# Turning the experts' hidden layer on its side: through memory, or block by block out of PSUM

## Chip, cores and metric

The kernel runs on one core of one Trainium2 chip. The metric is the device time of one execution in microseconds (us); the kernel before takes 285.71 us in the median of three runs (285.37 to 286.24).

## What is computed

A graph layer and a mixture of experts follow one another over 625 nodes of width 1024. The graph layer gathers neighbours by relation, projects them, applies an ELU, projects back and adds the result. The change touches only the mixture of experts:

```python
x = x + gnn(layernorm(x), edges, ...)
xf = layernorm(x)                                   # 625 x 1024
sh = gelu(xf @ sW1[i] + sb1[i]) @ sW2[i] + sb2[i]   # 2 shared experts, their mean
gates = xf @ rW + rb                                # 8 experts, the best 2 for each row
h = gelu(xf @ W1[e] + b1[e])                        # hidden width 256
y = h @ W2[e] + b2[e]
x = x + mean(sh) + sum_e w[t, e] * y[e, t]          # w: softmax over the best 2
```

## The kernel before, in words

All of it is one program whose instruction order on each engine is laid out ahead of time by the planner of the framework: of the instructions whose inputs it holds to be ready, it takes the earliest in program order. `tc.issue_after(a)` puts what is issued inside it behind `a` on `a`'s engine.

The graph layer fills the first 119 us. Then come the shared experts' first products (p_sh, L1146), with gating and routing between them. Routing sorts the chosen (row, expert) pairs into 11 tiles of 128 slots. In order of work the tiles are 4, 5, 6, 0, 7, 1, 8, 2, 9, 10, 3; below, "the first" to "the eleventh" tile counts in this order. Tiles 4 to 10 belong to one expert each. Tiles 0, 1 and 2 are split in two halves of 64 slots, tile 3 in four quarters of 32, with an expert for each part.

For each tile the loop `for s in range(NJ + 2)` (L1557) does this:

- `gather` (GpSimd) fetches 128 rows of 1024 from memory into one of three buffers, with four transfers for the tiles in `by_quarters` (first, second, fourth, sixth, eighth, tenth) and one for the others.
- `fetch` and `turn` bring the features to the partitions (xsT, two buffers). For the tiles in `by_quarters`, VectorE turns the whole tile at once (L1485). For the others TensorE turns it in two halves of four blocks (p_x, L1496); ScalarE evicts the first half (L1502), VectorE the second (L1500). The second half belongs to the next pass of the loop.
- `copy_w1` (ScalarE, L1509) copies first-layer weights for the split tiles.
- `expert_in` multiplies (p_h, L1515): 8 blocks of features, traced as 16 matmuls for a whole tile. The result is 128 slots by 256 hidden values in one PSUM bank; three banks serve these. The first four blocks need only the first half of xsT, the last four also the second.
- VectorE copies p_h to `hj` in SBUF, one buffer (L1519). SyncE's queue sends hj to `hd` in memory (L1521), and, with the next tile, four transfers of 32 KB bring it back to `hjT` (`to_quarters`, L1528), which moves each block of 32 hidden values to its own quarter of the partitions.
- `expert_mid`, at pass s for the tile s - 4, lets VectorE turn the 32x32 blocks inside each quarter (hT, L1537) and ScalarE apply bias and GELU back into hjT (L1542). L1537 is put behind the last copy of p_h.

`expert_out` (p_yj, L1578) multiplies the hidden values by W2, 512 columns to a PSUM bank, in the order 4, 5, 6, 0, 1, 2, 3, 7, 8, 9, 10. Its first two banks stand ahead of the closing of the pools `xts` and `in_w`; the other tiles follow in a loop with the copies of second-layer weights for split tiles (w2m, ScalarE, L1608), the evictions (ys, L1618 on VectorE and L1620 on ScalarE) and the scatters into `yt` (GpSimd, L1625). The last three `expert_mid` stand in that loop. On SyncE's queue, the loads of the shared experts' second weights (sw2, L1592) stand behind the last write of hd, then `to_quarters` of the last two tiles, then the loads of x1 (L1599).

Last come the shared experts' second products (p_o, L1676 and L1678), the weighted sums on VectorE (L1647) and the stores.

Of the kernel before, what the change touches and what calls it, by code (L numbers as in the profile page):

```python
# [8 lines left out]
F32 = mybir.dt.float32  # L9
# [14 lines left out]
H = 256  # L24
NE = 8
NS = 2
TP = 125
# [16 lines left out]
NJ = 11  # L44
# [9 lines left out]
HK = H // 128  # L54
# [399 lines left out]
def sparse_kernel(  # L454
# [24 lines left out]
    nc = tc.nc  # L479

    def pool(stack, name, bufs=1, side="left", **kw):
        return stack.enter_context(tc.tile_pool(name=name, bufs=bufs, side=side,
                                                reuse_waits="tile", **kw))
# [5 lines left out]
    dram = ctx.enter_context(tc.tile_pool(name="dram", bufs=1, space=bass.MemoryType.DRAM))  # L489
    h2d = dram.tile([N, D], F32, name="h2d")  # L490
    x1d = dram.tile([N, D], F32, name="x1d")
    hd = dram.tile([NJ, 128, H], F32, name="hd")

    yt = dram.tile([2 * YB, D], F32, name="yt")

    def ps_acc(name):
        return psum[0].tile([128, 512], F32, tag="acc", name=name, bufs=nacc[0])

    def ps_mm(name):
        return psum[0].tile([128, 512], F32, tag="mm", name=name, bufs=3)  # L500
# [279 lines left out]
    def first_row():  # L780
        x0 = xh[:TP, 0, :]
        h = rows.tile([TP, D], F32, tag="h", name="h_0")
        part = fbig.tile([TP, 3], F32, name="part")
        with tc.issue_after(behind.ins):
            nc.vector.tensor_reduce(part[:, 0:1], x0[:, :HALF], axis=AX.X, op=ALU.add)
        with tc.issue_after(table.ins):
            nc.scalar.activation(h[:, HALF:], x0[:, HALF:], AF.Identity, accum_out=part[:, 1:2])
        last = nc.vector.tensor_scalar(part[:, 2:3], part[:, 0:1], part[:, 1:2], -1.0 / D, op0=ALU.add, op1=ALU.mult)
        moved = nc.scalar.activation(h[:, :384], x0[:, :384], AF.Identity, bias=part[:, 2:3])
        with tc.issue_after(last.ins):  # L790
            last = nc.vector.tensor_scalar(h[:, 384:], x0[:, 384:], part[:, 2:3], None, op0=ALU.add)
        hs[0] = h
        return last, moved
# [264 lines left out]
    last, moved = first_row()  # L1058
# [122 lines left out]
    def load_w2(e):  # L1181
        nc.sync.dma_start(w2a[:, e], W2[e].rearrange("(k p) d -> p k d", p=128))
# [261 lines left out]
    mid = pool(ctx, "mid")  # L1444
    hjT = mid.tile([128, NJ, HK, 128], F32, name="hjT")
    xts = ExitStack()
    xt = pool(xts, "xt", 2, side="right")
# [5 lines left out]
    def parts(j):  # L1453
        if j < NH2:
            return (0, HS, e_of[j]), (HS, 128, e_of[NH2 + j])
        if j < NM2:
            return [(QS * i, QS * (i + 1), e_of[nt + i]) for i in range(4)]
        return ((0, 128, e_of[NH2 + j - 1]),)

    xsT, w1m, copied, moved = {}, {}, [], []  # L1460
    acts = []

    rows = {}
# [29 lines left out]
    def turn(j, g):  # L1493
        p = ps_acc(f"p_x{g}_{j}")
        for k in range(4):
            nc.tensor.transpose(p[:, k * 128 : (k + 1) * 128], half_row[j][:, 4 * g + k :: KD], ident)  # L1496
        o = xsT[j][:, 4 * g : 4 * g + 4, :]
        pv = p.rearrange("p (k n) -> p k n", k=4)
        if g:
            turned.append(nc.vector.tensor_copy(o, pv))  # L1500
        else:
            acts.append(nc.scalar.copy(o, pv))  # L1502
# [8 lines left out]
    def expert_in(j):  # L1511
        p = ps_mm(f"p_h_{j}")
        for k in range(KD):
            for a, b, e in parts(j):
                nc.tensor.matmul(p[a:b, :H], xsT[j][:, k, a:b],  # L1515
                                 w1m[j, a][:, 0, k, :] if a else w1a[:, bass.ds(e, 1), k, :],
                                 start=(k == 0), stop=(k == KD - 1))
        h = xt.tile([128, H], F32, tag="hj", bufs=1, name=f"hj_{j}")
        copied.append(nc.vector.tensor_copy(h.rearrange("p (q c r) -> p c q r", q=4, c=HK),  # L1519
                                           p[:, :H].rearrange("p (c q r) -> p c q r", c=HK, q=4)))  # L1520
        moved.append(nc.sync.dma_start(hd[j], h))  # L1521
        if j not in (tiles[0], tiles[-1]):
            with tc.issue_after(moved[-1].ins):
                to_quarters(tiles[tiles.index(j) - 1])

    def to_quarters(j):
        for q in range(4):
            nc.sync.dma_start(hjT[32 * q : 32 * q + 32, j].rearrange("t c (b r) -> t (c b r)", b=4)  # L1528
                              .rearrange("t (b x) -> t b x", b=4),
                              hd[j].rearrange("(b t) (q x) -> q t b x", b=4, q=4)[q])  # L1530

    bT = vT[:, KD + NS * HK :].rearrange("p (e t) -> p e t", t=HK)

    def expert_mid(j):
        p = mid.tile([128, HK, 128], F32, tag="hT", name=f"hT_{j}")
        with tc.issue_after(copied[-1].ins):
            nc.vector.transpose(p.rearrange("p c (b t) -> p c b t", b=4),  # L1537
                                hjT[:, j].rearrange("p c (b r) -> p (c b r)", b=4)
                                .rearrange("p (b c r) -> p c b r", b=4, c=HK))
        for t in range(HK):  # L1540
            for a, b, e in parts(j):
                done = nc.scalar.activation(hjT[:, j, t, a:b], p[:, t, a:b], AF.Gelu,  # L1542
                                     bias=bT[:, bass.ds(e, 1), t])
        acts.append(done)
# [3 lines left out]
    tiles = (*whole[:3], 0, whole[3], 1, whole[4], 2, *whole[5:], NH2)  # L1548
# [8 lines left out]
    for s in range(NJ + 2):  # L1557
        if 0 < s <= NJ and tiles[s - 1] in half_row:
            turn(tiles[s - 1], 1)
        if s < NJ:  # L1560
            if s > 2:
                rows[tiles[s]] = io.tile([128, D], F32, tag="io", name=f"xs_{tiles[s]}")
                gather(tiles[s])
            fetch(tiles[s])
        if 0 <= s - 1 < NJ:
            expert_in(tiles[s - 1])
        if s == 2:
            load_w2(NE - 1)
        if 0 <= s - 4 < NJ - 3:
            expert_mid(tiles[s - 4])  # L1570
    ORDER = (*whole[:3], *range(NM2), *whole[3:])
    w2m, p_ys = {}, {}

    def expert_out(j, s):
        p_ys[j, s] = p = ps_acc(f"p_yj_{j}_{s}")
        for k in range(HK):
            for a, b, e in parts(j):
                made = nc.tensor.matmul(p[a:b], hjT[:, j, k, a:b],  # L1578
                                        (w2m[j, a, k] if a else w2a[:, bass.ds(e, 1), k])[..., s * 512 : (s + 1) * 512],
                                        start=(k == 0), stop=(k == HK - 1))  # L1580
        return made

    for s in range(2):
        expert_out(ORDER[0], s)
    xts.close()
    in_w.close()

    late = pool(ctx, "late", side="right")
    sw2 = late.tile([128, NS, HK, D], F32, name="sw2")
    for i in range(NS):  # L1590
        with tc.issue_after(moved[-1].ins):
            last = nc.sync.dma_start(sw2[:, i], sW2[i].rearrange("(k p) d -> p k d", p=128))  # L1592
    with tc.issue_after(last.ins):
        to_quarters(tiles[-2])
        to_quarters(tiles[-1])
    x1 = late.tile([TP, NT, D], F32, name="x1")
    for a, b in ((0, 3), (3, NT)):
        with tc.issue_after(last.ins):
            nc.sync.dma_start(x1[:, a:b], x1d[a * TP : b * TP].rearrange("(t p) d -> p t d", p=TP))  # L1599
    gat = pool(ctx, "gat", 15, side="right")  # L1600

    loads, (off,) = nc.values_load_multi_w_load_instructions(flag, min_val=0, max_val=EC * 4 + 1)
# [7 lines left out]
    for n, j in enumerate(ORDER):  # L1610
        y = gat.tile([128, D], F32, tag="y", name=f"ys_{j}")
        for s in range(2):
            at = slice(s * 512, (s + 1) * 512)
            if n:
                made = expert_out(j, s)
            p = p_ys[j, s]
            if s or n < 4:
                copied.append(nc.vector.tensor_copy(y[:, at], p))  # L1618
            else:
                nc.scalar.copy(y[:, at], p)  # L1620

        if n < 3:
            expert_mid(tiles[n - 3])

        sent.append(nc.gpsimd.indirect_dma_start(  # L1625
            out=yt, out_offset=bass.IndirectOffsetOnAxis(ap=row[:, j : j + 1], axis=0), in_=y, in_offset=None,
            bounds_check=2 * YB - 1, oob_is_err=False))
        for s in sent[:-1]:
            tc.declare_no_dep(sent[-1].ins, s.ins, reason="rows of different slots")

    gs = {}
    for d in range(NT):
        for a in range(2):
            at = a * YB + 1 + d * TP
# [29 lines left out]
    for d in range(NT):  # L1664
        if LATE < d < NT - 1:
            add_rows(d)
        own = slice(d * TP, (d + 1) * TP)
        for at in ((0, 512), (512, D)) if d < NT - 1 else ((0, 512), (512, 768), (768, D)):
            n = at[1] - at[0]
            at = slice(*at)  # L1670
            p = (ps_mm if banks % 8 > 4 else ps_acc)(f"p_o_{d}_{at.start}")
# [59 lines left out]
```

## Time and profile before

| what | value |
|---|---|
| median of 3 runs | 285.71 us (285.37 to 286.24) |
| the profiled execution | 285.32 us, its span 283.5 us |
| granted TensorE clock | 0.997 of full speed |
| busy: TensorE matmul / VectorE / ScalarE / GpSimd | 274.4 / 175.7 / 101.8 / 61.1 us |
| instructions: matmul / VectorE / ScalarE / GpSimd | 1509 / 446 / 232 / 122 |
| p_h (L1515), first to last matmul | 158.37 to 203.8 us |
| hj copy (L1519) / hT turn (L1537) | 11 of 421 ns / 11 of 436 ns |
| DMA issues of SyncE for hd and hjT | 11 and 44 |

The span is the time between the first and the last instruction of the trace; 1.8 us lie around it. "Busy" is the time in which an engine had an instruction; matmuls overlap, and their ends are modelled. A "releaser" is what ended an engine's idle time. All positions are microseconds from the start of the span.

### The profile page before, as it was taken

How to read it: one execution, taken by the hardware profiler on the slowest of the kernel's cores; microseconds unless marked ns; L12 is line 12 of the kernel's file. 1: busy time of each engine (PE TensorE's matmuls, PEld its weight loads, DVE VectorE, ACT ScalarE, POOL GpSimd, SP SyncE). 2: the span in 40 equal slices, each digit the busy share in tenths (PEclk: the TensorE clock that was granted, in tenths of full speed). 3: DMA queues.
4: the chain of work that ended last, by engine and by line, in shares of the span. 5: the costliest groups of instructions: out<-in, count | busy, mean ns of one | idle time of the engine just before them, and what ended most of it. 6: DMA issues, size and time to landing. Idle time of an engine off the chain costs nothing.

```text
span 283.5 us, 4565 instructions
## 1 busy us (share of the span) xinstructions
PE 274.4 (97%) x1509; PEld 183.3 (65%) x1509; DVE 175.7 (62%) x446; ACT 101.8 (36%) x232; POOL 61.1 (22%) x122
## 2 busy tenths in 40 slices
PE   8899999999999999999999999799999999999993
PEld 7667777788888655677777787678544324444452
DVE  4889999999975689838930641555341312216972
ACT  2347326534642242445101150856298311100000
POOL 9810020000000032210047555360020222210000
PEclk9999999999999999999999999999999999999998
DMA  7999981000000899998999279754296554439962
GB/s 226 356 324 355 371 289 47 2 0 2 1 0 2 322 369 425 420 375 321 390 415 393 88 221 283 202 154 137 68 329 217 218 205 191 186 115 385 392 219 79
DMA packets 29987, 64.48 MB, mean 227 GB/s; under 512 B 8961, under 2 KB 16196, under 8 KB 28935
## 3 DMA queue, kind: packets, MB, share of 16 engines
q1 hardware_dynamic: 24475, 48.74, 47.9%
q0 software_dynamic: 5200, 15.04, 15.1%
q10 hardware_dynamic: 284, 0.35, 0.4%
q8 instruction: 14, 0.23, 0.3%
q14 instruction: 14, 0.11, 0.1%
HBM read 44.63 MB, written 20.26 MB: 229 GB/s over the span
## 4 chain that ended last, share of the span: by engine, by line
PE 82%; DMA 8%; DVE 7%; SPq 1%; issue 0%; ACT 0%; DVEq 0%
PE p_pr L956 15%; PE p_yj L1578 14%; PE p_o L1676 12%; PE p_sh L1146 12%; PE p_h L1515 10%; PE p_y L1031 6%; PE p_agg L985 5%; DMA xh<-in_x_dram 4%; DMA hd<-hj 4%; DVE st L777 2%; PE cnt L934 2%; PE p_t L844 2%; DVE ohs L903 1%; PE p_x L1496 1%; PE p_gate L1198 1%; PE p_y L1032 1%
## 5 line engine op out<-in xcount | busy, mean ns | idle before, releaser
L956 PE MATMUL p_pr<-wg,nT 128*125 128x286 f32 x240 | 62.4, 410 | 0.9 <-DVE neg L798 0.6
L956 PEld LDWEIGHTS p_pr<-wg,nT 128*125 128x125 f32 x240 | 43.3, 187 | 13.4 <-ACT nT L850 1.2
L1578 PE MATMUL p_yj<-w2a,hjT 128*128 (+2 forms) x88 | 38.7, 595 | 0.0
L1676 PE MATMUL p_o<-sw,shT 128*125 128x512 f32 (+1 forms) x88 | 36.3, 553 | 0.0
L1146 PE MATMUL p_sh<-h2T,sw 128*128 128x313 f32 (+1 forms) x128 | 35.3, 429 | 0.0
L1515 PE MATMUL p_h<-w1a,xsT 128*128 (+2 forms) x144 | 32.7, 380 | 1.5 <-DVE xsT L1485 1.5
L1578 PEld LDWEIGHTS p_yj<-w2a,hjT 128*128 128x128 f32 (+2 forms) x88 | 14.5, 168 | 23.3 <-issue 22.8
L1146 PEld LDWEIGHTS p_sh<-h2T,sw 128*128 128x128 f32 x128 | 23.6, 189 | 8.5 <-issue 0.2
L1515 PEld LDWEIGHTS p_h<-w1a,xsT 128*128 128x128 f32 (+2 forms) x144 | 22.8, 163 | 7.7 <-issue 1.7
L1676 PEld LDWEIGHTS p_o<-sw,shT 128*125 128x125 f32 x88 | 16.4, 187 | 16.9 <-issue 15.9
L1468 POOL DMA_INDIRECT xs<-h2d,tok x24 | 22.7, 946 | 19.0 <-issue 5.8
L1618 DVE COPY ys<-p_yj 128x512 f32<-128x512 f32 x15 | 10.3, 689 | 26.1 <-PE p_yj L1578 26.1
L1625 POOL DMA_INDIRECT yt<-ys,row x11 | 10.7, 970 | 48.9 <-DVE ys L1618 48.9
L1519 DVE COPY hj<-p_h 128x256 f32<-128x256 f32 x11 | 4.6, 421 | 24.5 <-PE p_h L1515 19.0
L1031 PE MATMUL p_y<-wo_t,eT 128*125 128x512 f32 (+1 forms) x40 | 18.8, 592 | 0.0
L1042 POOL DMA_DIRECT2D x1d<-xh x4 | 2.2, 542 | 65.6 <-DVE flagf L727 62.1
L1542 ACT ACTIVATE hjT<-hT,vT 128x128 f32<-128x128 f32 (+2 forms) x34 | 9.8, 354 | 17.1 <-DVE hT L1537 10.2
L985 PE MATMUL p_agg<-P,CT 125*125 125x288 f32 x100 | 15.5, 305 | 0.0
L1515 PE MATMUL p_h<-w1m,xsT 128*64 128x256 f32 (+1 forms) x96 | 14.7, 381 | 0.0
L1647 DVE SCALAR_TENSOR_TENSOR x<-g,wab,x 125x1024 f32<-125x1024 f32 (+1 forms) x12 | 13.2, 1105 | 1.9 <-DMA g<-yt 1.7
L1578 PE MATMUL p_yj<-w2m,hjT 128*64 128x512 f32 (+1 forms) x48 | 14.1, 595 | 0.0
L904 DVE TENSOR_TENSOR ohs<-ohs,cols 125x1024 f16<-125x1024 f16 (+1 forms) x22 | 14.0, 638 | 0.0
(306 smaller groups left out, 415.7 us busy)
## 6 DMA issues: line engine op xcount, KB each, us to landing
w1a<-in_L_ffn_W_dram SPq DMA_DIRECT2D x8, 1024.0 KB
w2a<-in_L_ffn_W_dram SPq DMA_DIRECT2D x8, 1024.0 KB
yt<-zero SPq DMA_DIRECT2D x2, 2560.0 KB
g<-yt SPq DMA_DIRECT2D x10, 512.0 KB
sw<-in_L_ffn_sW_dram SPq DMA_DIRECT2D x4, 1024.0 KB
h2d<-h POOLq DMA_DIRECT2D x5, 448.0 KB, 9.5
out_dram<-x SPq DMA_DIRECT2D x4, 448.0 KB
x<-x1d SPq DMA_DIRECT2D x1, 1500.0 KB
```

What stands on the lines that cost most here:

```text
L904: last = nc.vector.tensor_tensor(os, os, both(VV_, 128)[1], op=ALU.mult)
L956: product = nc.tensor.matmul(p[:TP, :F], nT[:, k, m * TP : (m + 1) * TP], wg[:, k, r, :], start=(k == 0), stop=(k == KD - 1))
L985: nc.tensor.matmul(p[:TP, : F + 2], CT[:, m, at : at + TP], P[:, m, r, i], start=(m == 0 and i == 0), stop=(m == NT - 1 and i == 1))
L1031: nc.tensor.matmul(ps[s][:TP, :], eT[:n, k, :], wo_t[:n, k, at], start=(k == 0), stop=False)
L1146: nc.tensor.matmul(p[:, : z - a], sw1[:, i, k, t * 128 : (t + 1) * 128], h2T[:, k, a:z], start=(k == 0), stop=(k == KD - 1))
L1468: nc.gpsimd.indirect_dma_start(out=rows[j][:, a * (D // 4) : (a + 1) * (D // 4)], out_offset=None, in_=h2d.rearrange("n (b f) -> (n b) f", ...
L1515: nc.tensor.matmul(p[a:b, :H], xsT[j][:, k, a:b], w1m[j, a][:, 0, k, :] if a else w1a[:, bass.ds(e, 1), k, :], start=(k == 0), stop=(k == ...
L1578: made = nc.tensor.matmul(p[a:b], hjT[:, j, k, a:b], (w2m[j, a, k] if a else w2a[:, bass.ds(e, 1), k])[..., s * 512 : (s + 1) * 512], star ...
L1618: copied.append(nc.vector.tensor_copy(y[:, at], p))
L1625: sent.append(nc.gpsimd.indirect_dma_start(out=yt, out_offset=bass.IndirectOffsetOnAxis(ap=row[:, j : j + 1], axis=0), in_=y, in_offset=No ...
L1647: added.append(nc.vector.scalar_tensor_tensor(*args, op0=ALU.mult, op1=ALU.add))
L1676: nc.tensor.matmul(p[:TP, :n], shT[:, i, k, own], sw2[:, i, k, at], start=(i == 0 and k == 0), stop=False)
```

## The change

The copy to hj, the way through memory and the turn of hjT go. In their place, `expert_in` issues 16 VectorE transposes for each tile. Each reads 32 partitions of the PSUM result (slots 32b to 32b+31) and, of two groups of 128 hidden values, the q-th 32, that is 64 values on each partition; it writes partitions 32q to 32q+31 of hT in SBUF. The inner loop is over q, the quarter that is written. hT has two buffers instead of one.

`expert_mid` is now the GELU alone, and it stands at pass s for the tile s - 2 instead of s - 4. The last two stand between the first two banks of `expert_out` and the closing of the pools. `hd`, `hj`, `to_quarters` and the lists that ordered them are gone, so on SyncE's queue the loads of sw2 and x1 have no such transfers ahead of them.

```diff
-    hd = dram.tile([NJ, 128, H], F32, name="hd")
@@ expert_in
-        h = xt.tile([128, H], F32, tag="hj", bufs=1, name=f"hj_{j}")
-        copied.append(nc.vector.tensor_copy(h.rearrange("p (q c r) -> p c q r", q=4, c=HK),
-                                           p[:, :H].rearrange("p (c q r) -> p c q r", c=HK, q=4)))
-        moved.append(nc.sync.dma_start(hd[j], h))
-        if j not in (tiles[0], tiles[-1]):
-            with tc.issue_after(moved[-1].ins):
-                to_quarters(tiles[tiles.index(j) - 1])
-
-    def to_quarters(j):
-        for q in range(4):
-            nc.sync.dma_start(hjT[32 * q : 32 * q + 32, j].rearrange("t c (b r) -> t (c b r)", b=4)
-                              .rearrange("t (b x) -> t b x", b=4),
-                              hd[j].rearrange("(b t) (q x) -> q t b x", b=4, q=4)[q])
+        h = mid.tile([128, HK, 128], F32, tag="hT", bufs=2, name=f"hT_{j}")
+        pv = p[:, :H].rearrange("p (c q r) -> p q c r", c=HK, q=4)
+        for b in range(4):
+            own = slice(32 * b, 32 * b + 32)
+            for q in range(4):
+                nc.vector.transpose(h[32 * q : 32 * q + 32, :, own], pv[own, q])
+        p_hs[j] = h
@@ expert_mid
-        p = mid.tile([128, HK, 128], F32, tag="hT", name=f"hT_{j}")
-        with tc.issue_after(copied[-1].ins):
-            nc.vector.transpose(p.rearrange("p c (b t) -> p c b t", b=4),
-                                hjT[:, j].rearrange("p c (b r) -> p (c b r)", b=4)
-                                .rearrange("p (b c r) -> p c b r", b=4, c=HK))
+        p = p_hs[j]
@@ the loop over s
-        if 0 <= s - 4 < NJ - 3:
-            expert_mid(tiles[s - 4])
+        if 0 <= s - 2 < NJ - 2:
+            expert_mid(tiles[s - 2])
@@ behind the first two banks of expert_out
+    for j in tiles[-2:]:
+        expert_mid(j)
@@ SyncE's queue
     for i in range(NS):
-        with tc.issue_after(moved[-1].ins):
-            last = nc.sync.dma_start(sw2[:, i], sW2[i].rearrange("(k p) d -> p k d", p=128))
-    with tc.issue_after(last.ins):
-        to_quarters(tiles[-2])
-        to_quarters(tiles[-1])
+        nc.sync.dma_start(sw2[:, i], sW2[i].rearrange("(k p) d -> p k d", p=128))
     for a, b in ((0, 3), (3, NT)):
-        with tc.issue_after(last.ins):
-            nc.sync.dma_start(x1[:, a:b], x1d[a * TP : b * TP].rearrange("(t p) d -> p t d", p=TP))
+        nc.sync.dma_start(x1[:, a:b], x1d[a * TP : b * TP].rearrange("(t p) d -> p t d", p=TP))
@@ the loop over the outputs
-                copied.append(nc.vector.tensor_copy(y[:, at], p))
+                nc.vector.tensor_copy(y[:, at], p)
-        if n < 3:
-            expert_mid(tiles[n - 3])
```

More of the change, by code (lines that the diff above doesn't have):

```diff
@@ L1458, in parts @@
         return ((0, 128, e_of[NH2 + j - 1]),)
-    xsT, w1m, copied, moved = {}, {}, [], []
+    xsT, p_hs, w1m = {}, {}, {}
     acts = []
```

## The prediction

> **What bounds the kernel now.** I read the page first, for the busy shares.
>
> ```profile
> span 283.5 us, 4565 instructions
> PE 274.4 (97%) x1509; PEld 183.3 (65%) x1509; DVE 175.7 (62%) x446; ACT 101.8 (36%) x232; POOL 61.1 (22%) x122
> ```
>
> TensorE (PE) is the bound: 274.4 of 283.5 us. A wait that TensorE doesn't feel is worth nothing; a wait that it comes to feel is paid in full, since nothing later gives it back. So I asked the view of waits where TensorE stands idle. From 140 us to the end it has one row for its matmuls:
>
> ```profile
> PE p_h L1515 <- DVE xsT L1485: 1.5, 1, 1.5
> ```
>
> The chain of waits tells where this is and what is behind it (start, length, what):
>
> ```profile
> 172.81 0.44 DVE hj L1519
> ...
> 173.26 3.74 DMA hd<-hj
> ...
> 177.10 0.06 DVE hj L1519
> ...
> 177.46 0.42 DVE hT L1537
> 177.87 1.95 DVE xsT L1485
> 179.82 0.14 issue
> 179.95 3.67 PE p_h L1515 x32
> ```
>
> The copy of the fifth result needs the only hj buffer, whose write to memory takes until 177.0. VectorE works in order, so the turn of the sixth tile's features (L1485) stands behind that copy, and TensorE waits for it from 178.44 to 179.95. This 1.5 us is all that the way through memory costs. Everywhere else its transfers lie beside products: their latency is hidden.
>
> **The budget that the change has to fit in.** TensorE needs features that VectorE makes: the second half of xsT (L1500) for the tiles that TensorE turns, and all of xsT (L1485) for the others. The timeline of VectorE in the steady part shows one pair of tiles:
>
> ```profile
> 191.82 0.42 DVE L1519 COPY hj<-p_h 128x256 f32<-128x256 f32 x1 [3.28 <-PE p_h L1515]
> 192.16 0.43 DVE L1537 STREAM_TRANSPOSE hT<-hjT 128x256 f32<-128x256 f32 x1
> 192.52 0.65 DVE L1500 COPY xsT<-p_x 128x512 f32<-128x512 f32 x1
> 193.10 2.04 DVE L1485 STREAM_TRANSPOSE xsT<-xs 128x1024 f32<-128x1024 f32 x1
> 195.91 0.42 DVE L1519 COPY hj<-p_h 128x256 f32<-128x256 f32 x1 [0.78 <-PE p_h L1515]
> ```
>
> A result's copy starts when its product ends. L1519 frees VectorE after 0.34, L1537 after 0.36, L1500 after 0.58, and then comes L1485. The next pair's first copy is at 199.81, so the pair takes TensorE 8.0 to 8.15 us (183.66 to 191.82 to 199.81). Of these VectorE uses some 4.0.
>
> In the changed kernel the 16 transposes of a tile take the place of L1519, ahead of L1500 and L1485 of the tiles behind it: they are earlier in the program and ready as soon as the product ends, while L1500 still waits for p_x. Call the time of the 16 **T**. TensorE's second half of a product (the weight load of its ninth matmul, 8 x 0.21 us after the first) comes 1.8 us after the copy's start for the third tile (166.00, load at 167.8), and some 2.0 us after it for the fifth, seventh, ninth and eleventh. L1500 lasts 0.65, and 0.11 passes from VectorE's end to TensorE's start (179.81 to 179.92). So a stall begins where T + 0.76 is over 1.8 to 2.05: **T of 1.04 to 1.3 us is free, and above that five tiles each pay the excess**, 5T - 6.1 us together.
>
> **What T is.** No row of this trace is a transpose of 64 values from PSUM into another quarter of the partitions. The turn L1537 lasts 0.436 for 256 values; at 1.04 ns each (0.69 against 0.42 for copies of 512 and 256 values) 0.267 of that are values and 0.169 are fixed. For 64 values: 0.067 + 0.169 = 0.236 us. What counts is how soon the next one starts, and the rows give two answers.
>
> ```profile
> 82.16 0.31 DVE L999 TENSOR_SCALAR lo<-agg 125x286 f32<-125x286 f32 x1
> 82.39 0.30 DVE L1002 TENSOR_SCALAR el<-agg 125x286 f32<-125x286 f32 x1
> ```
>
> ```profile
> 104.83 0.68 DVE L746 BATCH_NORM_STATS2 ln_1s<-xh 125x6 f32<-125x512 f32 x1
> 105.55 0.29 DVE L1019 TENSOR_TENSOR eR<-p_elT,eR 64x125 fp32r<-64x125 f32 x1
> 105.87 0.21 DVE L748 BATCH_NORM_AGGREGATE ln_1m<-ln_1s 125x2 f32<-125x12 f32 x1
> ```
>
> Independent instructions that begin at partition 0 overlap: L1002 starts 0.08 before L999 ends. L1019 reads and writes from partition 64: it starts 0.04 after the row before it has ended, and the row behind it 0.03 after its own end, in each of its five instances. So a change of the starting quarter costs the overlap. The change's inner loop writes another quarter with each of its 16 instructions. I take the second answer: 0.236 + 0.03 = 0.267, so **T = 4.27 us**. The other end: if writing elsewhere holds nothing, 64 values follow at 0.067 + 0.093 = 0.16 (L1537 frees VectorE after 0.36), T = 2.56; at the pitch of small plain instructions from PSUM (40 values each 0.12, so 64 at 0.14) T = 2.2. Above: at 0.30, between the estimate and L1019's 0.32 for 125 values, T = 4.8.
>
> [...]
>
> **The sum, with T = 4.27.** The first tile's set starts at 162.10 and ends at 166.37, so the second tile's set starts 0.37 late, at 166.37. From there VectorE is the bound. A pair costs it 2T + 0.60 + 2.0 = 11.14 us where TensorE had 8.15: set, L1500, L1485, set; the second half of the product waits for L1500 and ends about when L1485 does, so no set waits for TensorE. Four pairs (third to tenth tile) end at 166.37 + 44.56 = 210.93. The eleventh: a set 4.27, L1500 with signal 0.76, the second half of its product 1.83: p_h ends at 217.8 instead of 203.8, **14.0 us late**. The 1.5 us stall is inside this, replaced by longer ones.
>
> What TensorE can put in: p_yj of tile 4 is ready by then, 1.72 us a bank, but its PSUM banks are shared with p_x and, as the trace runs them (five banks of p_yj, then something else), are handed out in program order. So only the last stall, 3 us, can take it, to the extent that the planner foresees it: I take **-1.5**, bounds 0 and -3. What follows (75.05 us from 203.80 to the last matmul at 278.85, and the tail) keeps its length.
>
> Edits at nothing. The 55 transfers for hd and hjT leave SyncE's queue: 11 x 128 KB and 44 x 32 KB, which lie beside products now. The loads of sw2 need the space of w1a, so they start when p_h ends, as now (204.80); x1's loads come up to 7.9 us nearer to that (the last eight issues from 205.79), and their first use is beyond 250. The GELUs of the last two tiles (0.69 and 1.80) move ahead of the 12 copies w2m (11.44 us): the first split tile is the fourth in p_yj, behind six banks of 1.72, which cover it; uncovered it would cost 2.5. Two buffers of hT against GELUs of 0.69 to 1.80 in a tile's time make no wait. The last set (4.27) stands ahead of the ys evictions: five banks of p_yj give 8.6 us of cover.
>
> Profiled execution: 285.3 + 14.0 - 1.5 = **297.8 us**; the median of the runs, 285.7, is 0.4 above that execution, and I leave that inside the range.
>
> **Rivals.**
>
> - *Transposes overlap in spite of the new quarter.* T = 2.2 to 2.56: five stalls of 5T - 6.1 = 4.9 to 6.7 less the 1.5 that goes: 288.7 to 290.5. For it: no row shows the write side alone. Against: L1019. Near it in time is another: the planner puts L1500 and L1485 ahead of waiting transposes. Then 11 x 4.27 and 11.3 for features are 58 us of VectorE against 45 of stage, of which three banks of p_h let some 8 spill past the end: about 290.
> - *Faster: the wait for memory goes and nothing takes its place.* If a transpose frees VectorE after 0.075 (as the 8-value rows at 132 us do), T = 1.2 and no stall is left: 283.8. It decides at 5T - 6.1 = 1.5, T = 1.52, or 0.095 an instruction: 64 values alone are 0.067. Nothing that long is that short here.
> - *Within 0.3%* (0.86 us, about what a measurement can tell from no change): T of 1.35 to 1.7, a hundredth of a microsecond either way for each instruction.
> - *Worse:* PSUM as source or the turn's own fill adds to each: T of 4.8 gives 10 x 0.53 = 5.3 more, 303.1, and without filling 304.6.
>
> **Numbers.** Forecast 0.62 (293.5 to 302), overlap or another order 0.20 (288.7 to 292), worse than 303.5: 0.09, faster 0.06, same 0.03. The range, 288.7 to 303.5, takes in the first two. Faster 0.06, same 0.03, slower 0.91.
>
> **What would show it.** 176 transposes of some 0.24 us, each starting after the last has ended, 4.2 to 4.4 us a set; VectorE without gaps from 166 to 215; five TensorE waits of 3 us at p_h on L1500; p_h ending near 216 to 218. Wrong: starts 0.08 or more ahead of the last one's end (overlap), L1500 between transposes (order), or p_yj among the products p_h before the eleventh tile (filling).

## The result, and the profile after

| | before | after |
|---|---|---|
| median | 285.98 us (285.37 to 288.8, 6 runs) | 296.14 us (295.27 to 296.81, 6 runs) |
| ratio of the means | | 1.0337, 95% interval 1.029 to 1.0384 |
| profiled execution, its span | 285.32, 283.5 us | 295.3, 293.5 us |
| p_h, first matmul to the start of p_yj | 158.37 to 203.73 | 156.88 to 213.88 |
| from the last start of a p_h matmul to the end | 80.09 us | 79.94 us |

The change makes the kernel 3.4% slower. All of it arises between the first product of p_h and the first of p_yj: that stage grew from 45.36 to 57.00 us, 11.64. What lies behind it is as long as it was. What lies ahead came out 1.49 shorter, but nothing there was changed, and in all the kernels below p_h begins between 156.2 and 158.6: that is scatter. 11.64 - 1.49 - 0.15 = 10.0, the difference of the spans.

The page of the changed kernel: the span, the engines, and two rows of its costliest groups (line, engine, operation, result <- input, shape, count | busy in us, mean ns of one | idle time ahead of them and what ended most of it). Lines of the code have moved: the sets of transposes are L1522, the eviction L1500 is L1499 now, the turn L1485 is L1484, p_h is L1514.

```profile
span 293.5 us, 4581 instructions
...
PE 278.3 (95%) x1509; PEld 185.8 (63%) x1509; DVE 210.4 (72%) x600; ACT 102.0 (35%) x232; POOL 60.8 (21%) x122
...
L1522 DVE STREAM_TRANSPOSE hT<-p_h 32x64 f32<-32x64 f32 x176 | 43.3, 246 | 5.2 <-issue 1.2
...
L1514 PE MATMUL p_h<-w1a,xsT 128*128 (+2 forms) x144 | 36.4, 411 | 9.3 <-DVE xsT L1484 7.1
```

TensorE does the same 1509 matmuls in a longer span. VectorE at 72% does not look like a bound; the share is an average over the program. The view of one stretch tells more. First the p_h stage of the kernel before, then that of the changed one (stretch; length, then busy us and instructions of PE, PEld, DVE, ACT, POOL; granted TensorE clock; DMA share; GB/s):

```profile
158.40:203.70 45.30, 43.79 (x312) 34.99 (x312) 19.37 (x27) 21.06 (x48) 18.89 (x20) 1.00 0.60 172
```

```profile
156.90:213.90 57.00, 47.74 (x314) 37.06 (x313) 51.09 (x165) 23.02 (x54) 18.85 (x20) 0.94 0.30 93
```

VectorE had 19 us to do in 45, and now has 51 in 57; TensorE is idle for 9 us, DMA's share is halved, and that halving buys nothing. The granted clock of 0.94 is a second finding, taken up below. The view of waits has these two rows of TensorE for p_h, where there was one of 1.5:

```profile
PE p_h L1514 <- DVE xsT L1484: 7.1, 3, 2.8
PE p_h L1514 <- DVE xsT L1499: 2.2, 1, 2.2
```

And VectorE's timeline shows what TensorE waits behind (start, length, line, operation, shape, count):

```profile
176.90 0.69 DVE L1499 COPY xsT<-p_x 128x512 f32<-128x512 f32 x1
177.51 4.14 DVE L1522 STREAM_TRANSPOSE hT<-p_h 32x64 f32<-32x64 f32 x16
181.68 2.03 DVE L1484 STREAM_TRANSPOSE xsT<-xs 128x1024 f32<-128x1024 f32 x1
183.74 4.14 DVE L1522 STREAM_TRANSPOSE hT<-p_h 32x64 f32<-32x64 f32 x16
187.90 0.69 DVE L1499 COPY xsT<-p_x 128x512 f32<-128x512 f32 x1
189.31 4.15 DVE L1522 STREAM_TRANSPOSE hT<-p_h 32x64 f32<-32x64 f32 x16 [0.71 <-ACT hjT L1531]
193.49 2.03 DVE L1484 STREAM_TRANSPOSE xsT<-xs 128x1024 f32<-128x1024 f32 x1
```

A set takes 4.14 us, and the next instruction follows 0.03 after it: 0.26 for each of the 16. Sets, evictions and turns stand without a gap but for 0.71; TensorE has no work since 181.47, the turn L1484 begins behind the set at 181.68, and TensorE starts at 183.85.

### The profile page after: what moved, and what is told of

It is laid out like the page before. It is cut to its first block, busy times and chain, and to the rows that moved or that the text cites. A ratio compares the mean times of both kernels' runs of the same rounds, so it can differ in the third digit from the quotient of the medians.

```text
span 293.5 us, 4581 instructions
## 1 busy us (share of the span) xinstructions
PE 278.3 (95%) x1509; PEld 185.8 (63%) x1509; DVE 210.4 (72%) x600; ACT 102.0 (35%) x232; POOL 60.8 (21%) x122
## 5 line engine op out<-in xcount | busy, mean ns | idle before, releaser
L1522 DVE STREAM_TRANSPOSE hT<-p_h 32x64 f32<-32x64 f32 x176 | 43.3, 246 | 5.2 <-issue 1.2
L1514 PE MATMUL p_h<-w1a,xsT 128*128 (+2 forms) x144 | 36.4, 411 | 9.3 <-DVE xsT L1484 7.1
L1514 PEld LDWEIGHTS p_h<-w1a,xsT 128*128 128x128 f32 (+2 forms) x144 | 24.2, 174 | 18.5 <-issue 10.3
L1531 ACT ACTIVATE hjT<-hT,vT 128x128 f32<-128x128 f32 (+2 forms) x34 | 10.4, 355 | 28.9 <-DVE hT L1522 28.9
L1514 PE MATMUL p_h<-w1m,xsT 128*64 128x256 f32 (+1 forms) x96 | 17.0, 411 | 0.0
L1630 DVE SCALAR_TENSOR_TENSOR x<-p_o,x 125x512 f32<-125x512 f32 (+1 forms) x11 | 7.0, 641 | 10.7 <-PE p_o L1661 10.3
```

The source lines that it names most:

```text
L1514: nc.tensor.matmul(p[a:b, :H], xsT[j][:, k, a:b], w1m[j, a][:, 0, k, :] if a else w1a[:, bass.ds(e, 1), k, :], start=(k == 0), stop=(k == ...
L1522: nc.vector.transpose(h[32 * q : 32 * q + 32, :, own], pv[own, q])
L1630: added.append(nc.vector.scalar_tensor_tensor(*args, op0=ALU.mult, op1=ALU.add))
```

## The experiments

The theory to be tested: (1) each of the 16 transposes is held until the last has ended because it writes another quarter of the partitions than the one before; (2) the sum of VectorE's work in the stage sets its end. The rivals: for (1), that small transposes out of PSUM are slow in themselves, that only a new quarter on the read side holds, or that a transpose is slow when it writes another quarter than it reads; for (2), that it is the order on VectorE (features queued behind sets), or the half clock of TensorE (0.50 granted in two stretches of the stage), not the sum.

### The loops swapped: q_outer

```diff
-        for b in range(4):
-            own = slice(32 * b, 32 * b + 32)
-            for q in range(4):
+        for q in range(4):
+            for b in range(4):
+                own = slice(32 * b, 32 * b + 32)
                 nc.vector.transpose(h[32 * q : 32 * q + 32, :, own], pv[own, q])
```

> Same 16 transposes a tile, the loop over the written quarter now outside: four in a row write one quarter, but each reads another one than the last. Theory (a transpose is held whenever the quarter that it reads or writes differs from the last): all 16 are held as before the swap, 0.24 to 0.25 us each with 0.01 between, a set of 4.15 us, time 295.3 to 296.8 us, as the changed kernel. Rival (only a new quarter on the side that is written holds): 12 of 16 follow after 0.14 to 0.16 us, a set of 2.7 to 3.0 us, time 285 to 288 us.

296.82 us (296.26 to 297.33), ratio 1.0434 (1.0392 to 1.0475). A set lasts 4.14, as before the swap, though three of four instructions now write the quarter of the one ahead and change only the one they read. In the set at 173.10 the first eight start 0.25 to 0.26 apart, and each lasts 0.24 to 0.25; in the changed kernel, where three of four change only the quarter they write, the starts of the set at 172.73 are 0.25 to 0.27 apart. So a new quarter on the read side holds as one on the write side does.

### The same number of small transposes, each in its own quarter: own_quarter

```diff
-                nc.vector.transpose(h[32 * q : 32 * q + 32, :, own], pv[own, q])
+                nc.vector.transpose(h[own, :, 32 * q : 32 * q + 32], pv[own, q])
```

> 16 transposes of the same size a tile, but each writes the quarter that it reads (the blocks are not moved across quarters, so the hidden values reach the wrong places). Read and written quarter change with every fourth only. Theory: 4 are held at 0.26 us, 12 follow after 0.13 to 0.16, a set of 2.6 to 3.0 us; TensorE's waits at the products p_h fall from 9.3 us to 0 to 2, time 284 to 287 us. Rival (a transpose of 64 values from PSUM costs 0.26 whatever the quarters): a set of 4.15 us, 295 to 297 us.

285.08 us (284.12 to 286.62), ratio 1.0018 (0.9986 to 1.005). The group of this kernel:

```profile
L1522 DVE STREAM_TRANSPOSE hT<-p_h 32x64 f32<-32x64 f32 x176 | 28.9, 214 | 5.2 <-ACT hjT L1531 2.5
```

One lasts 0.21 us, but 176 of them keep VectorE busy for 28.9 only: they overlap. A set with the step to the next instruction takes 2.70 (170.14 to 172.84), 0.17 an instruction; within a quarter the starts are 0.13 to 0.19 apart, at a new quarter 0.21 to 0.22, which is 0.01 after the last has ended. No transpose here moves anything across quarters, and it is still held at a new one; in the changed kernel the four of 16 that write the quarter they read start as late (0.25 to 0.27) as the other twelve. So it is the change from one instruction to the next that holds, not the crossing inside one. Same instructions, same source, same number: the changes of quarter are worth 1.47 us a set and the whole loss of the change. Its waits:

```profile
PE p_h L1514 <- DVE xsT L1484: 1.5, 3, 0.5
PE p_h L1514 <- DVE xsT L1499: 0.4, 1, 0.4
```

1.9 us, about the 1.5 that the way through memory had cost.

### One transpose for the whole tile: one_turn

```diff
-        for b in range(4):
-            own = slice(32 * b, 32 * b + 32)
-            for q in range(4):
-                nc.vector.transpose(h[32 * q : 32 * q + 32, :, own], pv[own, q])
+        nc.vector.transpose(h.rearrange("p c (b t) -> p c b t", b=4),
+                            p[:, :H].rearrange("p (c q r) -> p c q r", c=HK, q=4))
```

> One transpose of 128 partitions a tile straight from PSUM in place of the 16 (the blocks are not moved across quarters, so the hidden values reach the wrong places). Theory (the whole loss is the time of the sets on VectorE): a set of 0.40 us, no wait of TensorE at p_h, also not the 1.5 us of the kernel before: 283.5 to 284.5 us, granted clock 1.0 throughout p_h. Rival (part of the loss is from the moved GELUs, from the other order of SyncE's loads or from the planner's other order): 286 us or more.

282.73 us (282.17 to 283.55), ratio 0.9928 (0.9901 to 0.9955). TensorE has no wait left in p_h.

```profile
L1519 DVE STREAM_TRANSPOSE hT<-p_h 128x256 f32<-128x256 f32 x11 | 5.0, 450 | 25.8 <-PE p_h L1514 22.3
```

All 128 partitions at once take 0.45, against 4.14 for the same values in 16 pieces, and the turn of as many values out of SBUF in the kernel before (hT, L1537) took 0.44. So it is not PSUM as the source that made the sets slow; this is what freedom from memory would be worth if no value had to change its quarter.

### The old way with a second hj: two_hj

This is the kernel before with one edit; the second buffer is the space of the gate weights, unused by then.

```diff
-        h = xt.tile([128, H], F32, tag="hj", bufs=1, name=f"hj_{j}")
+        h = (rw_t.rearrange("p k e -> p (k e)") if tiles.index(j) % 2
+             else xt.tile([128, H], F32, tag="hj", bufs=1, name=f"hj_{j}"))
```

> The kernel before with a second buffer for hj, nothing else. Theory (the 1.5 us at 178 us come from the one buffer alone): the copy of the fifth result no longer waits, TensorE runs p_h without a gap, 284.0 to 284.5 us, ratio to before 0.994 to 0.996. Rival (the features of the sixth tile would be late anyway, or the next write to memory in the queue): 285.3 to 286 us, ratio 1.

282.92 us (282.09 to 283.82), ratio 0.9931 (0.9902 to 0.9959): faster than both kernels, and with one_turn within the scatter. The one wait of 1.5 us is gone; TensorE's only row for p_h is

```profile
PE p_h L1515 <- DVE xsT L1500: 0.2, 1, 0.2
```

So the 1.5 us stall was all that the way through memory cost, and one more buffer removes it with the transfers still there.

### Less on VectorE: act_evict

```diff
         if g:
-            turned.append(nc.vector.tensor_copy(o, pv))
+            acts.append(nc.scalar.copy(o, pv))
```

> The changed kernel with the second halves of the features (five evictions of 0.62 us of VectorE's time) on ScalarE. Theory (in this stage VectorE's queue is the bound, and p_h ends when what is queued ahead of the last features is done): eight sets of 4.16 and four turns of 2.04 stand ahead, 41.5 us from the first set's start, so the tenth tile's product starts some 4 us earlier than the 46.1 us after it in the changed kernel; 291 to 293 us. Rival (TensorE's own waits and half-clock stretches are the bound, and ScalarE's evictions come late): 295 to 297 us.

293.45 us (290.87 to 293.95), ratio 1.0269 (1.0235 to 1.0303), above the 291 to 293 that the theory asked for. The profiled execution (span 289.1) is the fastest of the five and has the full clock (1.00) in the whole stage. VectorE loses five evictions of some 0.61, and runs sets and turns without a gap from 164 to 214 us:

```profile
178.84 2.03 DVE L1484 STREAM_TRANSPOSE xsT<-xs 128x1024 f32<-128x1024 f32 x1
180.89 8.32 DVE L1522 STREAM_TRANSPOSE hT<-p_h 32x64 f32<-32x64 f32 x32
189.25 2.03 DVE L1484 STREAM_TRANSPOSE xsT<-xs 128x1024 f32<-128x1024 f32 x1
```

A pair takes 10.41 (178.84 to 189.25) instead of 11.0, and the stage 53.2 instead of 57.0. From the first set to the last turn are 39.6 us instead of 43.9, four evictions (2.4) and the gaps (1.87); behind the last turn 0.4 of it is lost again. This execution had no half clock in the stage and its span is still 5.6 us longer than that of the kernel before, so the half clock is not what makes the loss. In the runs the gain is 0.0068 of the time before, 1.9 us, with intervals that just overlap. It points the way the theory says and is short of proof by itself.

### Another order, the same sum: sets_behind

The sets of a tile are issued behind the features of the next two tiles.

```diff
+    def turn_h(j):
+        p = p_hs[j]
         h = mid.tile([128, HK, 128], F32, tag="hT", bufs=2, name=f"hT_{j}")
...
+                with tc.issue_after(features[-1].ins):
                     nc.vector.transpose(h[32 * q : 32 * q + 32, :, own], pv[own, q])
...
-        if 0 <= s - 2 < NJ - 2:
-            expert_mid(tiles[s - 2])
+        if 0 <= s - 2 < NJ:
+            turn_h(tiles[s - 2])
+        if 0 <= s - 3 < NJ - 2:
+            expert_mid(tiles[s - 3])
```

> The changed kernel with each tile's set queued on VectorE behind the features of the next two tiles, never ahead of them. Theory (VectorE's sum is the bound): nine sets, five evictions and four turns still stand ahead of the last half of features, 48.7 us from the first set's start without gaps, so p_h ends at 53 to 56 us after the first p_h matmul instead of 57.0, 292.5 to 295.5 us. Rival (it was the order, sets ahead of features, that made TensorE wait): most waits go, 287 to 290 us.

293.14 us (292.06 to 294.24), ratio 1.0237 (1.0197 to 1.0276): the theory's figure. Now features go first, and VectorE runs without idle time, two sets between any two pairs of features:

```profile
175.91 0.69 DVE L1499 COPY xsT<-p_x 128x512 f32<-128x512 f32 x1
176.52 2.02 DVE L1484 STREAM_TRANSPOSE xsT<-xs 128x1024 f32<-128x1024 f32 x1
178.47 8.28 DVE L1528 STREAM_TRANSPOSE hT<-p_h 32x64 f32<-32x64 f32 x32
186.79 0.69 DVE L1499 COPY xsT<-p_x 128x512 f32<-128x512 f32 x1
187.39 2.04 DVE L1484 STREAM_TRANSPOSE xsT<-xs 128x1024 f32<-128x1024 f32 x1
```

A pair takes 10.88 (175.91 to 186.79), where it took 11.0 with the sets ahead. TensorE's waits are still 7.7 us, behind L1499. The order moves a wait from one line to another; it does not shorten the sum.

### TensorE kept busy in its waits: busy_pe, busy_wide5, busy_wide3

Whether the half clock costs time was to be seen by filling TensorE's waits with matmuls of ones; `ended[-1]` is the last matmul of the product ahead (for the third tile, of its first half).

```diff
         p = ps_mm(f"p_h_{j}")
+        if tiles.index(j) in (3, 5, 7, 9):
+            with tc.issue_after(ended[-1].ins):
+                for _ in range(24):
+                    nc.tensor.matmul(p[:, :128], hotc, hotc, start=True, stop=True)
...
```

> The changed kernel with 24 small matmuls without use, into the next result's bank, where TensorE waits for features (third, sixth, eighth and tenth tile). Theory (the granted clock halves after a stretch of some 3.4 us in which TensorE was idle for over 2 us): the clock stays at 1.0 through p_h, its matmuls take 380 ns on the mean instead of 411, and VectorE's gaps behind a product at half clock (1.2 us at 171.6) go: 293.5 to 295.5 us. Rival (the half clock has another cause than the waits): the 0.5 stretches stay, 411 ns, 296 us or more.

298.08 us (297.42 to 300.31), ratio 1.0414 (1.0375 to 1.0453): a miss, slower than the change itself by 2. The trace has three waits of TensorE for "issue" at 187.4 to 190.3 (2.4 us, with no engine as releaser; what held its instructions up is not shown), a half clock behind them (0.50 from 190.64 to 194.06), and 4.9 us without work on VectorE. Two more kernels did the same with 5 and with 3 matmuls of 512 columns at each place.

> Five bf16 matmuls of 128 x 512 (ones by ones) stand ahead of the first product of the fourth, sixth, eighth and tenth tile, in place of the 24 of 128 x 128 of the run before: 20 instructions more than the changed kernel, not 96, and some 1.1 us of TensorE work at each place. They go into the next result's bank, which that product starts anew, so the result is not touched. In the 24-matmul run TensorE waited 2.4 us for 'issue' in the middle of the eighth product, with VectorE, ScalarE and GpSimd idle too, and that is where its time went. Theory (VectorE's sum is the bound, nine sets ahead of the last eviction as in the changed kernel; the half clock only makes the VectorE gaps of 1.16 and 0.71): without that wait and without the half clock the time is the changed kernel's less at most 1.9, 294 to 296, ratio 1.028 to 1.035, and the granted clock is 1.0 wherever no idle of over 2 us is left in one 3.41 us piece. Rival (the added matmuls themselves delay the products that VectorE's next set needs): 297 or more with no wait for issue in the trace.

> The same with three matmuls of 128 x 512 at each place (0.65 us). Theory: idle pieces are about 0.5 longer than with five, so a half clock can come back; 294 to 296.5. Rival (the added matmuls cost by themselves): nearer to the changed kernel's 296 than the run with five, which would then be some 1 to 2 us slower than this one.

297.51 us (296.09 to 298.42), ratio 1.0441 (1.0379 to 1.0504), with five; 302.51 (300.41 to 303.77), ratio 1.0628 (1.0554 to 1.0702), with three. Both misses, and in the wrong order for the rival as well: fewer added matmuls cost more. All three still have stretches of half clock (0.50 for 3.42 us in busy_pe and in busy_wide5, for 6.84 and 3.40 in busy_wide3), so the question they were made for stays open. What they tell is something else. The added work changed the order that the planner lays out, and with it VectorE's idle time. VectorE from the start of its first set to the start of its last eviction into xsT (L1499, L1501 with the added lines):

| kernel | first set | last eviction | length | sets in between | VectorE idle | length less idle |
|---|---|---|---|---|---|---|
| sets_behind | 160.71 | 208.52 | 47.81 | 9 | 0.19 | 47.62 |
| q_outer | 160.28 | 210.30 | 50.02 | 9 | 1.84 | 48.18 |
| the change | 160.61 | 210.72 | 50.11 | 9 | 1.87 | 48.24 |
| busy_wide5 | 162.32 | 214.06 | 51.74 | 9 | 3.59 | 48.15 |
| busy_pe | 161.62 | 215.39 | 53.77 | 9 | 5.51 | 48.26 |
| busy_wide3 | 159.93 | 218.18 | 58.25 | 10 | 5.93 | 52.32 |

The last column is VectorE's own work, so it has to agree where the instructions do: 9 sets of 4.17, 4 evictions of 0.61, 4 turns of 2.06 make 48.2 (47.6 to 48.3 in the rows); with a tenth set 52.4. What tells is the column of idle time: 0.2 to 1.9 us in the first three kernels, so there VectorE's sum sets the end, and 3.6 to 5.9 in the three with added matmuls, so there idle time comes on top. In busy_wide3 the planner put ten sets ahead of the last features, and VectorE waits for products (1.78, 2.35 and 1.39 us):

```profile
175.27 0.69 DVE L1501 COPY xsT<-p_x 128x512 f32<-128x512 f32 x1
177.75 4.15 DVE L1530 STREAM_TRANSPOSE hT<-p_h 32x64 f32<-32x64 f32 x16 [1.78 <-remote]
181.93 2.03 DVE L1486 STREAM_TRANSPOSE xsT<-xs 128x1024 f32<-128x1024 f32 x1
183.99 4.13 DVE L1530 STREAM_TRANSPOSE hT<-p_h 32x64 f32<-32x64 f32 x16
190.48 4.15 DVE L1530 STREAM_TRANSPOSE hT<-p_h 32x64 f32<-32x64 f32 x16 [2.35 <-issue]
```

At the 1.78 no other set is ready: VectorE evicts, TensorE ends the product, and only then has VectorE something to turn. The 2.35 and the 1.39 stand behind products that ran for the most part at half clock (0.50 from 182.64 to 189.48 and from 209.96 to 213.36): the sixth tile's took from 184.02 to 190.37, 6.35 us, where the eighth tile's, split in the same way, takes 3.6 at full clock in the changed kernel (195.66 to 199.30). So the end of the stage is VectorE's sum plus whatever VectorE idles; the order and the clock count through that idle time, the order also through how many sets stand ahead of the last features. The stage behind it takes back little: from the last start of a p_h matmul to the end are 79.1 to 80.3 us in all these kernels.

## Why the prediction was right, and where its sizes were off

The direction, the mechanism and the size held: 297.8 forecast for the profiled execution, 295.3 measured; 296.14 in the median, inside the likeliest case. That the sum came so near is in part luck: two errors in it cancel, as shown below.

- **What bounds the kernel before, and what the way through memory costs.** Right: TensorE, and 1.5 us. One count is off: the copies to hj start at 162.10, 166.00, 172.81 and 177.10, so the one that the turn of the sixth tile stands behind is that of the fourth result, not of the fifth. two_hj removes this wait with a buffer and gains 0.7%, some 2 us; one_turn, without the transfers, gains no more. All else on SyncE's queue and in DMA was hidden, as costed: the stretch behind p_h is 79.94 us against 80.09.
- **T, the time of a set.** Right: 4.27 forecast, 4.17 measured with the step to the next instruction. The two prices stood as they were weighed. L1019's row, which begins 0.04 after the end of the one ahead, was read as a change of quarter that costs the overlap. It was thin evidence: L1019 changes both quarters at once, and the line has five semaphore instructions (21 ns each) beside its five rows. The runs decide it for reads and writes alike: 0.26 an instruction where the read or the write quarter changes each time (q_outer, the change), 0.13 to 0.19 where both stay (own_quarter).
- **VectorE as the bound.** Right: in the changed kernel VectorE idles 1.87 of 50.11 us, shorter sets take the loss away (own_quarter), and another order of the same work keeps it (sets_behind); act_evict points the same way. A pair was costed at 11.14 and takes 10.88 to 11.0.
- **The order on VectorE.** Wrong in part. Forecast: set, L1500, L1485, set all the way, with ten sets ahead of the last features and five waits of 3 us on L1500. From the fifth tile on the planner turns both halves of a TensorE-turned tile (p_x) ahead of the split tile's product, so the eviction is ready one set earlier, and nine sets stand ahead of the last one. There are four waits of 1.9 to 2.8, three of them on L1484. One set less is worth 4.17; busy_wide3, with ten, shows that it would have been paid. VectorE also wasn't without gaps: 1.87 us of idle, behind products in stretches with a granted clock of 0.50, for which the prediction has no term.
- **The fill, -1.5.** Wrong. TensorE put nothing of p_yj into its last wait: p_yj begins at 213.88, behind the last of p_h.
- **The end of p_h.** 217.8 forecast, 213.9 measured. From the one to the other: -1.49 for the earlier start, -4.27 for the set, -0.9 for the nine others (0.10 each), +0.3 for evictions and turns, +1.87 for the gaps, +0.57 for a tail of 3.16 instead of 2.59; that is 213.9. With the fill that did not come (+1.5) the errors partly cancel: 297.8 - 3.9 + 1.5 = 295.4. Without the fill the forecast would have been 4.0 too high, and 1.5 of that is only where p_h happened to begin.
- **The rival of overlap.** Its T, 2.2 to 2.56, is near what own_quarter has, 2.67. But its price was far too high: at five stalls of 5T - 6.1 it gave 288.7 to 290.5, and own_quarter, at T = 2.67, runs at the time of before, with four waits of 1.9 us together where the formula asks for 7.3. The step that failed is the free time, 1.04 to 1.3 us: it was read where L1500 stands behind the set, and the evictions of later tiles stand ahead of it. The budget of the pair, 2T + 2.6 against 8.15, would put the limit at T = 2.77; own_quarter fits it, and no run tries a T between 2.67 and 4.14.
- **The rival of the other order.** It gave about 290; sets_behind is that order and takes 293.14. Its two sets behind the last features, some 8 us, came as priced, but the change's own order has them too. What the price left out is that VectorE's first set begins 3.7 us into the stage and that 4.0 us of products follow the last eviction: 58 - 8.3 + 3.7 + 4.0 = 57.4, against 55.5 in sets_behind and 57.0 in the changed kernel.

## What to carry to other kernels

Before one wide VectorE instruction is replaced by many narrow ones, price the narrow ones by what frees the engine for the next, and look whether each starts in another quarter of the partitions than the last on either side: here that made the price 0.26 us instead of 0.13 to 0.19. A transfer that lay beside other work cost nothing here; if it stalls one instruction through a buffer, try a second buffer first. And compare the work of the two busiest engines within the stage, not over the program: a 72% engine was the bound.

## What the runs showed of the hardware

The granted TensorE clock fell to half in stretches of 3.40 to 3.42 us, once, in busy_wide3, of 6.84. Two of them are in the profile of the changed kernel; the first, by the microsecond (the columns as in the stretches above):

```profile
169.00:170.00 1.00, 0.31 (x1) 0.30 (x2) 1.00 (x2) 0.65 (x2) 0.86 (x1) 1.00 1.01 402
170.00:171.00 1.00, 1.00 (x5) 0.85 (x4) 1.00 (x1) 0.00 (x0) 0.84 (x1) 0.79 0.55 156
171.00:172.00 1.00, 1.00 (x3) 0.74 (x3) 0.58 (x1) 0.00 (x0) 0.25 (x2) 0.50 0.22 62
172.00:173.00 1.00, 1.00 (x4) 0.30 (x4) 0.25 (x2) 0.28 (x1) 0.79 (x1) 0.50 0.81 172
173.00:174.00 1.00, 1.00 (x8) 0.57 (x6) 0.95 (x4) 0.30 (x1) 0.91 (x1) 0.50 0.82 336
174.00:175.00 1.00, 1.00 (x12) 0.66 (x10) 0.96 (x4) 0.00 (x0) 0.69 (x2) 1.00 0.60 180
```

The clock, third from last, is 0.79 in the second row: full for 0.58 of that microsecond, then half. So it falls at 170.58 and is back at 174.0. TensorE had been idle from 167.5 to 169.69. The second stretch begins at 184.24, 13.66 later, four times 3.41. Within other traces the starts are 11 (q_outer, 37.54 us), 6 (sets_behind, 20.48) and 8 (busy_wide3, 27.32) times 3.41 apart; what sets these steps no run shows.

Counted in such steps from the falls of the same trace, the step ahead of a fall held 1.97 to 2.79 us of idle TensorE. No fall followed the waits of 1.91 and 2.79 us at 193.75 and 203.88 of the changed kernel, which the steps cut into 0.7 and 1.2 and into 0.8 and 1.95 (behind a wait of 2.79 that lies within one step of q_outer, from 203.46, the clock fell at 206.87), nor 2.03 us in a step of q_outer, nor the 1.5 us wait of the kernel before, whose stage has a clock of 1.00. The "over 2 us" that busy_pe was to test is an estimate that fits the changed kernel and q_outer: 2.12 to 2.79 ahead of their falls, at most 2.03 without one. busy_wide3 does not fit it: there a fall stands behind a step with 1.97, and the half clock goes on for a second step though the first held only 1.37 us of idle. In act_evict, which has no fall to count from, waits of up to 2.7 us left the stage at 1.00. So each fall came behind idle time of TensorE, and how much of it brings one on is not shown.

What this costs is bounded, not settled. In the changed kernel the first stretch slows the matmuls that a set waits for: the nine from 169.69 take 3.56 us, where in busy_wide5 and busy_wide3, at full clock, the same nine take 2.38 and 2.37. VectorE idles 1.16 us at 171.58; at full clock, in busy_pe and both busy_wide kernels, it idles 0.20 to 0.21 at that place. The other gap, 0.71, stands behind the product of the second stretch. An estimate of the cost from these gaps is 1.16 - 0.20 + 0.71, 1.7 us. All of VectorE's idle time in the stage is 1.87, so the half clock cannot cost more than that of the 10.0 us in that execution.
